# A fused attention and FFN layer: one up-projection chunk moved ahead of a down-projection, a root by GpSimd's power, an output scaled on ScalarE

## The chip, the core and the metric

The kernel runs on one core of a Trainium2 chip. A core has five engines that run side by side, each through its own queue of instructions: TensorE (PE in the profile; PEld is its weight load), VectorE (DVE), ScalarE (ACT), GpSimd (POOL) and SyncE (SP), which issues the transfers. [...]The metric is the device time of one execution in microseconds.

## The reference, cut to what matters

There are 8192 tokens (4 sequences of 2048) of 256 features. An attention in chunks of 32 tokens is followed by a feed-forward network (FFN) of 768 hidden features; after each, the input is added and the row is normalised.

```
Q, K, V = x @ W_q.T, x @ W_k.T, x @ W_v.T
S = (Q_chunk . K_chunk) * mask          # 32 x 32 in each chunk, decay ** (i - j) for i >= j
O = S @ V_chunk
attn = sigmoid(x @ W_g.T) * O @ W_o.T + x
h = layernorm(x + attn)                 # (r - mean) / sqrt(var + 1e-5)
u = silu(h @ wg.T) * (h @ wu.T)         # weights are integers / 127
out = layernorm(h + u @ wd.T)
```

## The kernel before, in words

The tokens go through in 16 blocks of 512, numbered 0 to 15. The FFN's products run in two parts whose sum keeps the precision: a "hi" part in a rounded fp32 type and a "lo" part in fp16, which holds the rest.

The FFN of a block has an up part and a down part. The up part (`ffn_up`, L775) goes by six chunks of 128 hidden features. For a chunk, TensorE makes the gate and the up product (`fg` and `fu`, L786) in two PSUM banks; ScalarE takes the sigmoid `s` (L794); VectorE multiplies the gate by it (L796) and the up product by that (`u`, L808); ScalarE casts `u` to its hi part (L810); GpSimd subtracts to give the lo part (L811). The tiles `s` and `u` have two buffers each, so the multiply of a chunk waits until the lo part of the chunk two before it is done. The down part (`ffn_down`, L823) multiplies the chunks with the down weights. In its `chunkwise` form (L852), used for blocks 13 and 14, the products of chunks 0 to 3 ("early") of both banks come first, then those of chunks 4 and 5 ("late"). Each bank is then added to `h` by VectorE (L834), which also takes mean and variance per row (L309, L310).

A normalisation needs 1/sqrt(variance + eps) for a block's four groups of 128 tokens, that is on a tile of 128x4. Most blocks take ScalarE's square root and VectorE's reciprocal. In three places `iterated_scale_and_shift` (L366) is used: for block 1's attention output (L936), for block 13's FFN output (L1033) and for block 14's (L1065). VectorE scales the variance (L382) and makes a first guess from its bits (L387, L391); GpSimd then refines it by ten chained operations and makes the shift by one more (L393 to L403). `normalize` (L406) applies scale and shift on ScalarE, one group of 128x256 per instruction; `by_vector` (L883) does it on VectorE.

The end of the kernel is written out by hand from L1037: up of block 14, its down (L1064), its root (L1065), then up of block 15. Two of the four groups of block 14's output are scaled by ScalarE beside chunks 3 and 4 of that (`up_beside`, L1051), the other two by VectorE after the last chunk (L1076). Chunks 4 and 5 of block 15 go by halves of 256 tokens (`cols`). Then ScalarE loads the square root's table (L1074), and the last down goes group by group (L1099): residual (L1119), mean and variance, root, scaling, store. Groups 0 and 1 are scaled by ScalarE, groups 2 and 3 by VectorE.

The order on an engine is the planner's choice, except between instructions passed to `in_turn` (and to `in_steady_turn` from block 1 to the last up part), which keep the order of the program among each other. Transfers are all issued in turn on SP's queue.

Of the kernel before, what the change touches and what calls it, by code (L numbers as in the profile page):

```python
# [47 lines left out]
F32 = mybir.dt.float32  # L48
F32R = mybir.dt.float32r
F16 = mybir.dt.float16  # L50
I32 = mybir.dt.int32
AF = mybir.ActivationFunctionType
ALU = mybir.AluOpType

P = 128
# [4 lines left out]
NG = TB // P  # L60
# [11 lines left out]
def kernel(  # L72
# [15 lines left out]
    nc = tc.nc  # L88
# [3 lines left out]
    KH = H // P  # L92
# [3 lines left out]
    const = ctx.enter_context(tc.tile_pool(name="const", bufs=1))  # L96
# [84 lines left out]
    make_identity(nc, ident)  # L181
    eps = const.tile([P, 1], F32, tag="eps", name="eps")
    nc.vector.memset(eps, EPS)


    m_sb = const.tile([P, KD, D], F32, tag="m", name="m_sb")
# [101 lines left out]
    def in_turn(ins):  # L288
        tc.keep_in_program_order(ins)
# [72 lines left out]

    def iterated_scale_and_shift(mv, kind, name):  # L366
        on_r, on_dst = kind

        def column(tag):
            return small.tile([P, NG], F32, tag=tag, bufs=2, name=f"{tag}_{name}")  # L370

        def times(out, a, b):
            nc.gpsimd.tensor_tensor(out, a, b, ALU.mult)

        def line(out, a, slope, at_0):
            nc.gpsimd.tensor_scalar(out, a, slope, at_0, ALU.mult, ALU.add)

        v, guess, y, t, q, minus, shift = map(
            column, ("v", "guess", "y", "t", "q", "minus_mean", "term")
        )  # L380
        in_turn(
            nc.vector.tensor_scalar(  # L382
                v, mv[:, :, 1], 1 / on_dst**2, EPS * (on_r / on_dst) ** 2, ALU.mult, ALU.add
            )
        )
        in_turn(
            nc.vector.tensor_scalar(  # L387
                guess, v.bitcast(I32), -0.5, float(0x5F3759DF), ALU.mult, ALU.add
            )
        )  # L390
        in_turn(nc.vector.tensor_copy(y.bitcast(I32), guess))  # L391
        nc.gpsimd.tensor_scalar(minus, mv[:, :, 0], -1.0, None, ALU.mult)
        times(t, y, y)  # L393
        times(t, t, v)
        line(q, t, 0.375, -1.25)
        times(q, q, t)
        line(q, q, 1.0, 1.875)
        times(y, y, q)
        times(t, y, y)
        times(t, t, v)  # L400
        line(t, t, -0.5, 1.5)
        times(y, y, t)
        times(shift, y, minus)  # L403
        return y, shift
# [370 lines left out]
    def ffn_up(b, hT, uT, chunks, cols=slice(0, TB), held=False, order=free):  # L775

        n = cols.stop - cols.start
        for hc in chunks:
            pg = bank(f"fg_{b}_{hc}_{cols.start}")[:, :n]
            pu = bank(f"fu_{b}_{hc}_{cols.start}")[:, :n]  # L780

            kinds = (0, 1) if hc % 2 == 0 else (1, 0)
            for kind in kinds:
                for pb, w in ((pg, fg), (pu, fu)):
                    for dc in range(KD):
                        nc.tensor.matmul(  # L786
                            pb,
                            lhsT=w[kind][:, dc, hc * P : (hc + 1) * P],
                            rhs=hT[kind][:, dc, cols],
                            start=(kind == kinds[0] and dc == 0),  # L790
                            stop=(kind == kinds[1] and dc == KD - 1),
                        )
            s = work.tile([P, n], F32, tag="s", name=f"s_{b}_{hc}")
            order(nc.scalar.activation(s, pg, AF.Sigmoid, scale=SCALE / H_UP))  # L794

            gated = nc.vector.scalar_tensor_tensor(  # L796
                s, pg, U_UP / H_UP**2, s, ALU.mult, ALU.mult
            )
            in_steady_turn(gated)
            if len(uT[0]) == hc:  # L800
                for kind, dtype, tiles in zip(("hi", "lo"), (F32R, F16), uT):
                    tiles.append(
                        acts.tile([P, TB], dtype, tag=f"u_{kind}", name=f"u_{kind}_{b}_{hc}")
                    )

            def multiply(hc=hc, pu=pu, s=s):
                u = work.tile([P, n], F32, tag="u", name=f"u_{b}_{hc}")
                in_steady_turn(nc.vector.tensor_tensor(u, pu, s, ALU.mult))  # L808
                hi, lo = uT[0][hc][:, cols], uT[1][hc][:, cols]
                nc.scalar.copy(hi, u)  # L810
                nc.gpsimd.tensor_tensor(lo, u, hi.bitcast(F32), ALU.subtract)  # L811

            if held:
                return multiply
            multiply()
# [7 lines left out]
    def ffn_down(b, uT, h, between=None, chunkwise=False):  # L823


        r = work.tile([P, NG, D], F32, tag="r2", name=f"r2_{b}")
        mv = no_moments(f"f{b}")
        made = None
        order = in_turn if chunkwise else free

        def residual(gs, pb):

            order(
                nc.vector.scalar_tensor_tensor(  # L834
                    flat(r, gs), pb, SCALE**3 / U_UP * H_UP, flat(h, gs), ALU.mult, ALU.add
                )
            )
            nonlocal made
            moments(r, f"f{b}", range(gs.start, gs.stop), order, mv)
            if between is not None and gs.start == 0:  # L840
                made = between()

        ws = [chunked(w) for w in fd]
        if chunkwise:
            per = TB // D
            banks = [bank(f"fdn_{b}_{k}") for k in range(NG // per)]
            for late, terms in enumerate(early_and_late(uT, ws)):
                for k, pb in enumerate(banks):
                    for i, (part, w) in enumerate(terms):
                        for j in range(per):  # L850
                            g = k * per + j
                            product = nc.tensor.matmul(  # L852
                                pb[:, j * D : (j + 1) * D],
                                lhsT=part[:, g * P : (g + 1) * P],
                                rhs=w,
                                start=late + i + j == 0,
                                stop=True,
                                skip_group_check=True,
                            )
                            in_turn(product)  # L860
                    if late:
                        residual(slice(k * per, (k + 1) * per), pb)
        else:
            project_back(b, uT, ws, residual, "fdn")
        return r, mv, made
# [17 lines left out]
    def by_vector(r, g, mv, std):  # L883
        in_turn(
            nc.vector.tensor_scalar(
                r[:, g, :],
                r[:, g, :],
                mv[:, g, 0:1],
                std[:, g : g + 1],
                ALU.subtract,  # L890
                ALU.mult,
            )
        )
# [4 lines left out]
    hs, hTs = {}, {}  # L898
    sg, v = attn_gate(0), attn_v(0)
# [26 lines left out]
    v, rest = split_v(2, x_sums)  # L926
# [15 lines left out]
    scales_out = r_out = None  # L942
# [5 lines left out]
    for b in range(NB - 2):  # L948
# [6 lines left out]
        yT, v, sg = ahead  # L955
# [38 lines left out]
        r_before = r_out  # L994
# [39 lines left out]

    last = NB - 1  # L1037
    per = NG // 2
    cols = [slice(i * per * P, (i + 1) * per * P) for i in range(2)]
# [3 lines left out]
    def store_groups(b, r, groups):  # L1043
        tokens = slice(b * TB + groups[0] * P, b * TB + (groups[-1] + 1) * P)
        dst = out[tokens, :].rearrange("(g p) d -> p g d", p=P)
        in_turn(nc.sync.dma_start(dst, r[:, groups[0] : groups[-1] + 1, :]))

    def up(b, uT, *chunks):
        ffn_up(b, hTs[b], uT, range(*chunks))

    def up_beside(b, uT, hc, r, groups, cols=slice(0, TB)):  # L1051

        multiply = ffn_up(b, hTs[b], uT, range(hc, hc + 1), cols, held=True)
        normalize(r, *scales_out, groups)
        multiply()
# [5 lines left out]
    up_beside(last - 1, uT, 4, r_out, range(per, NG))  # L1061
    store(last - 2, r_out)
    up(last - 1, uT, 5, KH)
    r_before, mv_before, _ = ffn_down(last - 1, uT, hs[last - 1], chunkwise=True)  # L1064
    scales_out = iterated_scale_and_shift(mv_before, of_out, f"out_{last - 1}")  # L1065
    up(last, uT_last, 0, KH - 3)
    up_beside(last, uT_last, KH - 3, r_before, range(0, 1))
    up_beside(last, uT_last, KH - 2, r_before, range(1, per), cols[0])
    store_groups(last - 1, r_before, range(0, per))
    ffn_up(last, hTs[last], uT_last, range(KH - 1, KH), cols[0])  # L1070
    ffn_up(last, hTs[last], uT_last, range(KH - 2, KH), cols[1])
    steady = False

    in_turn(nc.scalar.activation(table, eps, AF.Sqrt))  # L1074
    for g in range(per, NG):
        by_vector(r_before, g, mv_before, scales_out[0])  # L1076
    store_groups(last - 1, r_before, range(per, NG))
    r = work.tile([P, NG, D], F32, tag="r2", name=f"r2_{last}")

    def by_scalar(r, g, std, shift):  # L1080
# [168 lines left out]
```

## Time and profile before

Three runs took 529.88 to 529.99 us, the median 529.95. The profile is of one execution on the chip.

| what | us |
|---|---|
| median of three runs | 529.95 |
| the profiled execution | 529.89 |
| its span | 528.1 |
| TensorE busy in the span | 517.7 |
| VectorE busy | 390.9 |
| GpSimd busy | 343.3 |
| ScalarE busy | 321.7 |
| last product of the last down starts | 519.86 |
| last scaling on VectorE starts, takes | 522.63, 0.41 |
| subtraction for a lo part, 128x512 on GpSimd | 1.28 |
| an operation on 128x4 on GpSimd | 0.20 |

Times inside the span count from its start. A line of a timeline gives the start, the time from the first start to the last end, the engine, the line of the program, the operation, the tile written and those read, and how often; in brackets stands how long the engine was idle before it and what ended that. A line of the chain gives start, length, engine, tile and line. An engine that is idle costs time only where the chain goes through it.

### The profile page before, as it was taken

The page shows a single profiled execution, that of the slowest core. Times are in us where ns is not written, and L with a number is a line of the kernel's source. Part 1 is how long each engine was busy: PE and PEld are TensorE (multiplying, and loading weights), DVE is VectorE, ACT ScalarE, POOL GpSimd, SP SyncE. Part 2 cuts the span into 40 slices and gives each one's busy share as a digit, 9 for nine tenths or more (in the row PEclk, how much of TensorE's full clock was granted, in tenths as well). Part 3 has the DMA queues.
Part 4 walks back from the last instruction along what each step waited for, and adds up shares of the span by engine and source line. Part 5 has one row for each costly group of instructions (what it writes and reads, how often), then busy time and mean ns, then how long its engine had stood idle before and what let it go on. Part 6 is the DMA issues. An engine that isn't in the chain of part 4 may idle for free.

```text
span 528.1 us, 10574 instructions
## 1 busy us (share of the span) xinstructions
PE 517.7 (98%) x3646; PEld 422.0 (80%) x3646; DVE 390.9 (74%) x971; ACT 321.7 (61%) x642; POOL 343.3 (65%) x491
## 2 busy tenths in 40 slices
PE   8999999999999999999999999999999999999993
PEld 5798887887978788887887978788887887968773
DVE  3778797686786867777686786867777686788775
ACT  2745565475656656666575656656666575667653
POOL 6535785767848668585767848668585767644752
PEclk9999999999999999999999999999999999999998
DMA  7621120213212131130313213131140312012101
GB/s 254 216 89 41 52 69 21 61 44 92 68 36 85 56 106 40 45 117 24 97 46 86 73 36 85 56 106 40 42 120 21 99 46 78 1 35 86 42 20 63
DMA packets 43256, 36.90 MB, mean 70 GB/s; under 512 B 4800, under 2 KB 39104, under 8 KB 43200
## 3 DMA queue, kind: packets, MB, share of 16 engines
q1 hardware_dynamic: 42240, 35.41, 22.7%
q10 hardware_dynamic: 960, 0.79, 0.4%
q8 instruction: 30, 0.49, 0.4%
q14 instruction: 26, 0.21, 0.1%
HBM read 20.45 MB, written 8.39 MB: 55 GB/s over the span
## 4 chain that ended last, share of the span: by engine, by line
PE 92%; DVE 4%; POOL 1%; ACT 1%; issue 1%; DVEq 0%; ACTq 0%
PE fg L786 16%; PE fu L786 15%; PE fdn L673 14%; PE p_v L472 9%; PE p_y L454 9%; PE p_g L454 9%; PE p_o L472 8%; PE po L647 5%; PE ps L626 3%; PE pa L673 1%; POOL u_lo L811 1%; PE pg L568 1%; PE pi L178 1%; PE pv L606 1%; PE py L585 1%
## 5 line engine op out<-in xcount | busy, mean ns | idle before, releaser
L811 POOL TENSOR_TENSOR u_lo<-u,u_hi 128x512 f16<-128x512 f32 (+1 forms) x98 | 123.1, 1257 | 110.7 <-ACT u_hi L810 109.1
L810 ACT CAST u_hi<-u 128x512 fp32r<-128x512 f32 (+1 forms) x98 | 59.7, 609 | 67.3 <-DVE u L808 66.9
L796 DVE SCALAR_TENSOR_TENSOR s<-fg,s 128x512 f32<-128x512 f32 (+1 forms) x98 | 65.8, 672 | 33.3 <-ACT s L794 33.1
L794 ACT ACTIVATE s<-fg 128x512 f32<-128x512 f32 (+1 forms) x98 | 57.0, 583 | 42.0 <-PE fg L786 41.8
L808 DVE TENSOR_TENSOR u<-fu,s 128x512 f32<-128x512 f32 (+1 forms) x98 | 66.4, 679 | 12.3 <-POOL u_lo L811 2.2
L786 PE MATMUL fg<-hT_hi,fg_hi 128*128 128x512 f32 (+1 forms) x196 | 74.0, 458 | 0.0
L786 PE MATMUL fu<-hT_hi,fu_hi 128*128 128x512 f32 (+1 forms) x196 | 60.5, 390 | 0.0
L786 PE MATMUL fg<-hT_lo,fg_lo 128*128 128x512 f16 (+1 forms) x196 | 58.0, 377 | 0.0
L786 PE MATMUL fu<-hT_lo,fu_lo 128*128 128x512 f16 (+1 forms) x196 | 57.4, 375 | 0.0
L673 PE MATMUL fdn<-fd_hi,u_hi 128*128 128x256 f32 x312 | 46.8, 292 | 0.0
L786 PEld LDWEIGHTS fu<-hT_hi,fu_hi 128*128 128x128 f32 x196 | 36.5, 188 | 8.5
L786 PEld LDWEIGHTS fg<-hT_hi,fg_hi 128*128 128x128 f32 x196 | 34.5, 189 | 8.8
L409 ACT ACTIVATE h<-h,shift_h,scale_h 128x256 f32<-128x256 f32 x52 | 27.0, 590 | 23.7 <-POOL shift_h L360 23.7
L673 PEld LDWEIGHTS fdn<-fd_hi,u_hi 128*128 128x128 f32 x312 | 39.8, 189 | 0.3
L673 PE MATMUL fdn<-fd_lo,u_lo 128*128 128x256 f16 x312 | 38.6, 273 | 0.0
L786 PEld LDWEIGHTS <-fu_lo 128*128 128x128 f16 x196 | 19.2, 98 | 22.2
L834 DVE SCALAR_TENSOR_TENSOR r<-fdn,h 128x512 f32<-128x512 f32 x30 | 20.7, 689 | 21.6 <-PE fdn L673 19.1
L769 POOL TENSOR_TENSOR hT_lo<-hT,hT_hi 128x512 f16<-128x512 f32 x28 | 35.2, 1279 | 1.2 <-ACT hT_hi L768 1.2
L786 PEld LDWEIGHTS <-fg_lo 128*128 128x128 f16 x196 | 15.3, 98 | 20.9 <-issue 12.9
L673 PEld LDWEIGHTS <-u_lo 128*128 128x128 f16 x312 | 28.4, 98 | 4.2
L472 PE MATMUL p_v<-v_sums,x_sums 128*128 128x128 f32 x240 | 31.7, 275 | 0.0
L647 PE MATMUL po<-sT,v 128*128 128x128 f32 x256 | 31.2, 275 | 0.0
(217 smaller groups left out, 1183.9 us busy)
## 6 DMA issues: line engine op xcount, KB each, us to landing
x<-in_x_dram SPq DMA_DIRECT2D x16, 512.0 KB, 3.5
xT<-in_xT_dram SPq DMA_DIRECT2D x15, 512.0 KB, 4.3
hT<-sq SPq DMA_DIRECT2D x224, 32.0 KB, 1.9
out_dram<-r SPq DMA_DIRECT2D x14, 512.0 KB, 5.0
fg_int<-in_ffn_gT_dram SPq DMA_DIRECT2D x3, 256.0 KB, 8.2
fu_int<-in_ffn_uT_dram SPq DMA_DIRECT2D x3, 256.0 KB, 6.9
fd_int<-in_ffn_dT_dram SPq DMA_DIRECT2D x3, 256.0 KB, 5.9
xT<-in_xT_dram SPq DMA_DIRECT2D x2, 256.0 KB, 4.1
```

What stands on the lines that cost most here:

```text
L409: nc.scalar.activation(r[:, g, :], r[:, g, :], AF.Identity, bias=shift[:, g : g + 1], scale=scale[:, g : g + 1],)
L454: nc.tensor.matmul(pb, lhsT=a[i - 1], rhs=b[i - 1], start=first, stop=True, skip_group_check=True,)
L472: nc.tensor.matmul(pb[:, g * P : (g + 1) * P], lhsT=b[i - 1][:, g * P : (g + 1) * P], rhs=a[i - 1], start=first and g == 0, stop=True, ski ...
L647: nc.tensor.matmul(po[:, cols], lhsT=v[:, g, dc * P : (dc + 1) * P], rhs=sT[:, cols], start=True, stop=True,)
L673: nc.tensor.matmul(pb[:, j * D : (j + 1) * D], lhsT=part[:, g * P : (g + 1) * P], rhs=w, start=(i == 0), stop=(i == len(terms) - 1),)
L769: nc.gpsimd.tensor_tensor(in_order[1], whole, in_order[0].bitcast(F32), ALU.subtract)
L786: nc.tensor.matmul(pb, lhsT=w[kind][:, dc, hc * P : (hc + 1) * P], rhs=hT[kind][:, dc, cols], start=(kind == kinds[0] and dc == 0), stop=( ...
L794: order(nc.scalar.activation(s, pg, AF.Sigmoid, scale=SCALE / H_UP))
L796: gated = nc.vector.scalar_tensor_tensor(s, pg, U_UP / H_UP**2, s, ALU.mult, ALU.mult)
L808: in_steady_turn(nc.vector.tensor_tensor(u, pu, s, ALU.mult))
L810: nc.scalar.copy(hi, u)
L811: nc.gpsimd.tensor_tensor(lo, u, hi.bitcast(F32), ALU.subtract)
```

## The change

Three things change. Chunk 0 of block 15's up part is issued before block 14's down part instead of after it. In `iterated_scale_and_shift`, the bit guess and one refinement step of six GpSimd operations are replaced by one GpSimd instruction, a power with exponents from a constant tile of −0.5; one Newton step of four operations stays. And all four groups of block 14's output are scaled by ScalarE: groups 0 and 1 beside chunk 3, group 2 beside the first half of chunk 4, group 3 beside that of chunk 5; VectorE no longer scales any, and the second store follows ScalarE. The planner also moves two instructions on ScalarE and VectorE near block 15's transposition.

```
+    half = const.tile([P, NG], F32, tag="half", name="half")
+    nc.vector.memset(half, -0.5)
...
-        v, guess, y, t, q, minus, shift = map(
-            column, ("v", "guess", "y", "t", "q", "minus_mean", "term")
+        v, y, t, minus, shift = map(
+            column, ("v", "y", "t", "minus_mean", "term")
         )
...
-        in_turn(
-            nc.vector.tensor_scalar(
-                guess, v.bitcast(I32), -0.5, float(0x5F3759DF), ALU.mult, ALU.add
-            )
-        )
-        in_turn(nc.vector.tensor_copy(y.bitcast(I32), guess))
+        nc.gpsimd.tensor_tensor(y, v, half, ALU.pow)
         nc.gpsimd.tensor_scalar(minus, mv[:, :, 0], -1.0, None, ALU.mult)
-        times(t, y, y)
-        times(t, t, v)
-        line(q, t, 0.375, -1.25)
-        times(q, q, t)
-        line(q, q, 1.0, 1.875)
-        times(y, y, q)
         times(t, y, y)
         times(t, t, v)
         line(t, t, -0.5, 1.5)
...
+    up(last, uT_last, 0, 1)
     r_before, mv_before, _ = ffn_down(last - 1, uT, hs[last - 1], chunkwise=True)
     scales_out = iterated_scale_and_shift(mv_before, of_out, f"out_{last - 1}")
-    up(last, uT_last, 0, KH - 3)
-    up_beside(last, uT_last, KH - 3, r_before, range(0, 1))
-    up_beside(last, uT_last, KH - 2, r_before, range(1, per), cols[0])
+    up(last, uT_last, 1, KH - 3)
+    up_beside(last, uT_last, KH - 3, r_before, range(0, per))
     store_groups(last - 1, r_before, range(0, per))
-    ffn_up(last, hTs[last], uT_last, range(KH - 1, KH), cols[0])
+    for i in range(per):
+        up_beside(last, uT_last, KH - 2 + i, r_before, [per + i], cols[0])
+    store_groups(last - 1, r_before, range(per, NG))
     ffn_up(last, hTs[last], uT_last, range(KH - 2, KH), cols[1])
...
-    for g in range(per, NG):
-        by_vector(r_before, g, mv_before, scales_out[0])
-    store_groups(last - 1, r_before, range(per, NG))
```

## The prediction

> **What bounds the kernel now.** I read the shares of busy time and the chain of work first, then the chain's last 60 us in order of time, then the timeline of single engines there.
>
> ```profile
> PE 517.7 (98%) x3646; PEld 422.0 (80%) x3646; DVE 390.9 (74%) x971; ACT 321.7 (61%) x642; POOL 343.3 (65%) x491
> PE 92%; DVE 4%; POOL 1%; ACT 1%; issue 1%; DVEq 0%; ACTq 0%
> ```
>
> TensorE sets the time, and its work does not change. Only its gaps and what follows its last product can be won: from 484.6 us (the start of block 14's up chunks) to the end. The chain there:
>
> ```profile
> 499.57 0.63 ACT u_hi L810
> 500.20 0.07 issue
> 500.27 1.28 POOL u_lo L811
> 501.55 0.05 issue
> 501.60 1.33 PE fdn L852 x10
> ...
> 513.58 1.29 POOL u_lo L811
> 514.87 0.02 issue
> 514.90 0.42 DVE u L808
> ...
> 517.03 0.90 DVE r L885 x2
> 517.93 0.34 DVE r L1119
> ```
>
> TensorE waits for the lo part of block 14's chunk 5; later VectorE waits for GpSimd to free a buffer, and two scalings of block 14's output stand on VectorE just before the last block's first residual, L1119. Around the first wait, TensorE:
>
> ```profile
> 499.99 0.77 PE L852 MATMUL fdn<-fd_hi,u_hi 128*128 128x256 f32 x4
> 500.60 0.39 PE L852 MATMUL fdn<-fd_lo,u_lo 128*128 128x256 f16 x2
> 501.60 0.39 PE L852 MATMUL fdn<-fd_lo,u_lo 128*128 128x256 f16 x2 [0.61 <-POOL u_lo L811]
> ...
> 502.68 0.71 PE L786 MATMUL fg<-hT_hi,fg_hi 128*128 128x512 f32 x2
> ```
>
> Block 13's same 16 products took from 482.77 to 484.63 (1.86 us start to start); these took 2.69. So the stall is 0.83 us, not the 0.61 listed[...]. GpSimd afterwards:
>
> ```profile
> 505.79 0.22 POOL L392 TENSOR_SCALAR minus_mean_out<-mv_f 128x4 f32<-128x4 f32 x1 [4.25 <-DVE mv_f L310]
> 506.40 0.20 POOL L373 TENSOR_TENSOR t_out<-y_out 128x4 f32<-128x4 f32 x1 [0.39 <-DVE y_out L391]
> ...
> 509.20 0.20 POOL L373 TENSOR_TENSOR term_out<-y_out,minus_mean_out 128x4 f32<-128x4 f32 x1
> 509.35 2.54 POOL L811 TENSOR_TENSOR u_lo<-u,u_hi 128x512 f16<-128x512 f32 x2
> ```
>
> Two lo parts start the moment the root is done: the root holds the queue that the chain's later waits end on.
>
> [...]lo parts with finished casts sat behind the root[...]. [...]0.275 us a step of the root against rows of 0.20. [...]
>
> **The change, part by part.** *Chunk ahead.* Chunk 0 of block 15 (1.81 us on TensorE, from chunk 2's starts at 506.37 and 508.18) goes before block 14's down. The lo part of chunk 5 landed at 501.55; its reader would now come at 500.79+1.81=502.60, so 1.05 us of cover replace the stall: **−0.83 us on TensorE**. If that cover is used up, the stall returns. TensorE reaches chunk 1 at 503.66 and the last down at 512.80 (was 513.63). VectorE's pair for chunk 0 (0.60+0.82) fits into the 2.48 us it sat idle before L834, its lo part (1.28) into GpSimd's 4.25 idle. But block 14's residual is pushed back: L834 at 502.02−0.83+1.81=503.00, and L382 at 505.74+0.98=506.72. Queued behind it on VectorE: chunk 1.
>
> *Root.* Leave: L387, L391 on VectorE, and six of eleven chained GpSimd steps. L382 to the end of the last step took 505.74→509.40=3.66 us. Now: 0.24 to the power, the power P, 0.07, five steps of 0.275: 1.69+P. P is in no trace. Lower bound: the nearest row, 0.20. [...]**I take 0.5**[...]. Then the root ends at 508.9. There are three roots; block 1's (L936) ended at 58.55, and now near 55.8+P, used by ScalarE at 58.92: nothing up to P=3. The token sums interleaved with it come P plus about 0.7 later, against a first reader at 56.62: hidden below P=2.7. Block 13's ended at 491.87, would end at 489.9+P; the lo parts behind it have GpSimd's later gaps (0.21, 0.75, 0.69, 0.41) and the 1.05 of cover. The constant (one 128x4 memset at setup) lies under the first loads.
>
> *ScalarE alone.* Two L885 leave VectorE: 517.03→517.85, **−0.82** directly before L1119. ScalarE gains two scalings of 0.50 ahead of the last casts. Between 509.77 and 517.57 it idled 0.56+0.79+0.50 us, while its casts waited for VectorE, so they mostly fit. Both stores of that output go out earlier on SP; nothing else is in SP's way.
>
> *The end, step by step* (starts by the rows' spacing, in the changed kernel's instruction order). VectorE starts chunk 1 at 506.82 (was 507.65: guess, cast and chunk 0 stood before it). Its multiply ends at 508.33; cast 508.36; lo part 509.05 to 510.3. ScalarE then: s of chunk 3 at 508.88, scaling 509.37, cast of chunk 2 at 509.87, scaling, s of chunk 4, cast of chunk 3 at 511.2. Lo parts: chunk 2 at 510.55, chunk 3 at 511.87 to 513.15 (was 514.87). The multiply of chunk 5's first half follows at 513.25 (was 514.90). From there to the last multiply it was 1.79; I add 0.11 for ScalarE's scalings: 515.15 (was 516.69). L1119 0.34 later at 515.49 (was 517.85): 2.36 earlier, 1.54 by the multiplies and 0.82 by L885. The square-root table can load only after the last cast (515.6 to 516.0), until 517.2; the first root follows at 517.33, and group 2's residual, behind its reciprocal, at 517.69 instead of 517.53: −0.16. TensorE: the last down took 6.62 (513.63→520.25) with stalls of 0.53 and 0.38, so 512.80+5.71 plus 0.15 for a late lo part ends at 518.66, just before VectorE reads group 3 at 518.74. The rest is unchanged. **Sum: 2.36−0.16=2.20 us.** The profiled execution took 529.89 (span 528.1 and 1.79 around it); minus 2.20 is 527.69. The median is 0.06 above that run, so **527.7** after rounding down.
>
> **Rivals.** *The power is dear.* One mechanism: GpSimd's queue at the two late roots. Past P=0.8 block 14's root delays lo part 1 (0.6 free, 0.2 in a gap) one for one; past about 2.2 block 13's also uses up the cover and stalls TensorE, two for one. The gain is 2.2−1.4=0.8 at P=2.2 and nothing at P=2.6; from there it decides the sign. At 4 us: 2.2−1.4−3.6=−2.8, 532.7 us[...]. For: a power is unlike any row. Against: zero gain needs 2.6 us for four columns, (2.6−0.2)/(4×0.0021)=290 times a subtraction, whose slope is (1.28−0.20)/508=2.1 ns a column. *The power costs 1 to 2.6 us*: 528.0 to 529.9.
> *ScalarE becomes the bound.* If its last stretch had no slack, both scalings would delay the last cast by the full 1.0 us: gain 1.2, 528.7. For: they stand before the casts. Against: 1.85 us of idling there.
> *The wait moves.* The later residual (0.98) and a later root could take the place of the stall, so that the end does not move: 529.9. For: L382 does come later. Against: the root is 1.5 shorter and one chunk fewer queues behind it.
>
> **How the numbers follow.** Cheap power as summed: 0.62, own range 527.2 to 528.2. Power 1 to 2.6: 0.15. Dearer: 0.14. ScalarE: 0.05. Wait moves: 0.04. Below and above 0.2% (1.06 us, about what a measurement here can tell from no change, thus 528.89 and 531.01): faster 0.62+0.05+0.09=0.76; same 0.06+0.04+0.01=0.11; slower 0.13. The range, 527.1 to 530.0, takes in the power up to 2.6 us and leaves out the slow case and a few in 100 below.
>
> **What would show it.** Right: no gap in block 14's L852; the three powers under 0.8 us by start spacing; chunk 3's lo part ending near 513.1; ScalarE's table load near 515.9; the first L1119 near 515.5 and the last scaling ending near 520.8. Wrong: a power over 2.6 us with L811 late behind it; or L1119 waiting for TensorE; or VectorE's last pairs waiting for ScalarE.

## The result, and the profile after

The changed kernel took 528.34 us (median of 11 runs, 527.63 to 529.07), the kernel before 529.91 us on the same chip (11 runs, 529.22 to 531.08). The ratio is 0.9968 with a 95% interval of 0.9960 to 0.9976: 1.7 us faster, between 1.3 and 2.1. The forecast was 527.7 and a gain of 2.2.

The profiled execution took 527.63 us, its span 525.9. The page's busy times and the chain's shares of the kernel after:

```profile
PE 517.3 (98%) x3646; PEld 422.2 (80%) x3646; DVE 389.8 (74%) x964; ACT 322.3 (61%) x644; POOL 343.2 (65%) x476
PE 95%; DVE 2%; ACT 1%; POOL 1%; issue 0%; DVEq 0%; ACTq 0%
```

TensorE works as long as before (517.3 us, 517.7 before); its share of the chain went from 92 to 95%, VectorE's from 4 to 2%. What was won lies in gaps, as it had to. TensorE around the end of block 14's down, kernel after (start, length, engine, line, operation):

```profile
501.78 0.73 PE L842 MATMUL fdn<-fd_hi,u_hi 128*128 128x256 f32 x4
502.35 0.61 PE L842 MATMUL fdn<-fd_lo,u_lo 128*128 128x256 f16 x4
502.71 0.72 PE L842 MATMUL fdn<-fd_hi,u_hi 128*128 128x256 f32 x4
503.28 0.61 PE L842 MATMUL fdn<-fd_lo,u_lo 128*128 128x256 f16 x4
```

The lo products of chunks 4 and 5 now run as one group of four; the pause of 0.61 us in their middle is gone. GpSimd after that, where the root's size can be read:

```profile
506.76 0.23 POOL L388 TENSOR_SCALAR minus_mean_out<-mv_f 128x4 f32<-128x4 f32 x1 [4.24 <-DVE mv_f L312]
506.96 1.03 POOL L387 TENSOR_TENSOR y_out<-v_out,half 128x4 f32<-128x4 f32 x1
508.07 0.20 POOL L374 TENSOR_TENSOR t_out<-y_out 128x4 f32<-128x4 f32 x1
...
509.20 0.20 POOL L374 TENSOR_TENSOR term_out<-y_out,minus_mean_out 128x4 f32<-128x4 f32 x1
509.35 2.57 POOL L801 TENSOR_TENSOR u_lo<-u,u_hi 128x512 f16<-128x512 f32 x2
```

The power takes 1.03 us, not 0.5. The new root's first step, on VectorE, comes 0.97 us later than the old one's (506.71 and 505.74), behind the moved residual, the root is 0.97 us shorter (2.69 instead of 3.66), and so it ends at 509.40, just where the old one ended. What this queue gains is the chunk that no longer stands in it: of the two lo parts that start at 509.35, one is chunk 1's and the other chunk 2's; before, they were chunk 0's and chunk 1's. The chain in order of time shows that this queue is still on it, and that ScalarE has come onto it behind the queue (start, length, engine, tile, line):

```profile
502.99 0.70 DVE r L824
...
506.99 1.01 POOL y_out L387
...
509.20 0.20 POOL term_out L374
509.40 1.25 POOL u_lo L801
510.64 0.02 issue
510.67 0.70 DVE u L798
511.45 0.62 ACT u_hi L800
512.07 0.36 ACT r L399
...
512.48 0.36 ACT s L784
512.84 0.29 ACT u_hi L800
513.13 0.51 ACT r L399
513.64 0.28 ACT s L784
513.94 0.44 DVE s L786
...
515.38 0.44 DVE u L798
515.82 0.02 issue
515.84 0.41 ACT u_hi L800
```

The two rows of the tile r are scalings of block 14's output, two of the four that ScalarE now makes. The two queues are nearly level here: the multiply at 513.47, inside this stretch, still waited 0.18 us for a lo part. The multiply at 513.94 starts 0.47 us after it, where the same step in the next pair takes 0.34; so ScalarE costs 0.13 us here.

And VectorE's last run of work, kernel after: the four residuals of the last block, the reciprocal before the third, and the last scaling.

```profile
515.73 0.41 DVE L1109 SCALAR_TENSOR_TENSOR r<-fdn,h 128x256 f32<-128x256 f32 x1
...
516.74 0.39 DVE L1109 SCALAR_TENSOR_TENSOR r<-fdn,h 128x256 f32<-128x256 f32 x1
...
517.98 0.16 DVE L867 RECIPROCAL rstd_f<-rstd_f 128x1 f32<-128x1 f32 x1 [0.17 <-ACT rstd_f L320]
518.06 0.41 DVE L1109 SCALAR_TENSOR_TENSOR r<-fdn,h 128x256 f32<-128x256 f32 x1
...
519.11 0.41 DVE L1109 SCALAR_TENSOR_TENSOR r<-fdn,h 128x256 f32<-128x256 f32 x1
...
520.80 0.41 DVE L875 TENSOR_SCALAR r<-r,mv_f,rstd_f 128x256 f32<-128x256 f32 x1
```

The first residual came at 515.73 instead of 517.85, the last scaling at 520.80 instead of 522.63: 1.83 us earlier. The two profiled spans differ by 2.2. The rest of that pair, 0.37, comes after the last scaling: 528.1−523.04=5.06 us before, 525.9−521.21=4.69 after. The stores there are issued on SP, and in each profile one issue of the last few takes several times as long as the others. Durations in ns (minimum, median, maximum) of SP's stores from 517 us on, first the kernel before, then after:

```profile
L1046 SPq DMA_DIRECT2D out_dram<-r x5: 344/372/1594, 518.0 to 524.2; - x5
```

```profile
L1037 SPq DMA_DIRECT2D out_dram<-r x4: 333/344/1409, 519.2 to 521.2; - x4
```

Before, the long one is the third group's, so that the fourth store was issued only at 524.2; after, it is the fourth itself, issued at 521.2. One trace of each kernel can't tell whether this comes from the change. Two things speak for chance: the profiled execution was the fastest of the eleven (527.63, their median 528.34), and over all runs the gain is 1.7, near VectorE's 1.83.

### The profile page after: what moved, and what is told of

Its sections match the earlier page's. It is cut to its first block, busy times and chain, and to the rows that moved or that the text cites. A ratio compares the mean times of both kernels' runs of the same rounds, so it can differ in the third digit from the quotient of the medians.

```text
span 525.9 us, 10552 instructions
## 1 busy us (share of the span) xinstructions
PE 517.3 (98%) x3646; PEld 422.2 (80%) x3646; DVE 389.8 (74%) x964; ACT 322.3 (61%) x644; POOL 343.2 (65%) x476
## 4 chain that ended last, share of the span: by engine, by line
PE 95%; DVE 2%; ACT 1%; POOL 1%; issue 0%; DVEq 0%; ACTq 0%
PE fg L776 16%; PE fu L776 16%; PE fdn L663 14%; PE p_v L462 9%; PE p_y L444 9%; PE p_g L444 9%; PE p_o L462 8%; PE po L637 5%; PE ps L616 3%; PE fdn L842 2%; PE pa L663 1%; PE pg L558 1%; PE pi L178 1%; PE pv L596 1%; PE py L575 1%; DVE st_f L311 0%
## 5 line engine op out<-in xcount | busy, mean ns | idle before, releaser
L824 DVE SCALAR_TENSOR_TENSOR r<-fdn,h 128x512 f32<-128x512 f32 x30 | 20.7, 689 | 21.6 <-PE fdn L663 19.1
```

## The experiments

**How they are compared.** Thirteen profiles of nearly the same program show one more thing: where the time of two executions differs by chance. TensorE's first `p_g` product starts anywhere from 13.74 to 14.49 us; later the programs keep step. From the first product of an early down, at about 107.5, to that of block 13's down it is 107.57→478.95 in the kernel after, 107.94→479.32 with the scaling alone, 107.42→478.80 with the power alone: 371.38 us each time. So beside the measured ratio I give the start of VectorE's last scaling counted from block 14's first up product. The kernel before has 522.63−484.63=38.00, the kernel after 520.80−484.61=36.19. This leaves out the start, block 1's root, and the stores at the end. The measured differences have intervals of about ±0.4 to ±0.7 us, too wide for the small steps, so these are read from this count, and the ratio is its check. Each count comes from one execution; that a second one would give the same is not shown, only that equal stretches of different kernels take equal time.

| kernel | gain over before in us, 95% interval | last scaling, from block 14's first up product | against before |
|---|---|---|---|
| before | | 38.00 | |
| chunk ahead alone | 0.48 (0.11 to 0.79) | 37.56 | −0.44 |
| scaling by ScalarE alone | 0.37 (−0.05 to 0.85) | 37.60 | −0.40 |
| new root alone | 1.17 (0.74 to 1.59) | 36.91 | −1.09 |
| all but the new root | 1.06 (0.58 to 1.54) | 37.25 | −0.75 |
| all but the chunk ahead | 1.64 (1.01 to 2.23) | 36.54 | −1.46 |
| all but the scaling | 1.91 (1.17 to 2.65) | 36.60 | −1.40 |
| after | 1.70 (1.27 to 2.12) | 36.19 | −1.81 |

**One part alone.** The chunk ahead:

```
+    up(last, uT_last, 0, 1)
     r_before, mv_before, _ = ffn_down(last - 1, uT, hs[last - 1], chunkwise=True)
     scales_out = iterated_scale_and_shift(mv_before, of_out, f"out_{last - 1}")
-    up(last, uT_last, 0, KH - 3)
+    up(last, uT_last, 1, KH - 3)
```

> The chunk ahead alone, old root, two scalings left on VectorE. Theory (GpSimd's queue and VectorE's last run of work set the end): TensorE's stall of 0.83 us in block 14's down goes, but block 14's residual and so the root's end come 0.98 us later while only one lo part (1.28 us) fewer stands behind the root, so the lo part of chunk 3 and the end gain only about 0.3 to 0.6 us: some 529.4 against 529.9. Rival (TensorE's stall is the gain): 0.8 us or more, 529.1 or less, as TensorE is busy 98% of the span. Rival (the wait only moves): no gain, 529.9.

Measured: 529.48 against 529.99 us, ratio 0.9991 (0.9985 to 0.9998). TensorE's stall in block 14's down is gone, as in the kernel after, and yet the gain is about half of its 0.83 us. GpSimd's queue says why (chunk ahead alone):

```profile
510.48 0.20 POOL L373 TENSOR_TENSOR term_out<-y_out,minus_mean_out 128x4 f32<-128x4 f32 x1
510.62 2.55 POOL L811 TENSOR_TENSOR u_lo<-u,u_hi 128x512 f16<-128x512 f32 x2
513.44 1.97 POOL L811 TENSOR_TENSOR u_lo<-u,u_hi 128x512 f16<-128x512 f32 x2 [0.26 <-ACT u_hi L810]
```

Counted from block 14's first product (484.92 here), the root ends 0.99 us later than before, because block 14's residual was pushed back; the lo part of chunk 3 starts at 28.52 instead of 28.95. One lo part of 1.28 us less in the queue, 0.99 us of lateness more: that leaves 0.29 us, a shorter idle time before it adds the rest of the 0.43, and the end gets 0.44. TensorE, busy 98% of the span, is not what passes the gain on.

The new root (the power and one Newton step in place of the bit guess and a longer iteration):

```
-        in_turn(nc.vector.tensor_copy(y.bitcast(I32), guess))
+        nc.gpsimd.tensor_tensor(y, v, half, ALU.pow)
...
-        line(q, t, 0.375, -1.25)
-        times(q, q, t)
-        line(q, q, 1.0, 1.875)
-        times(y, y, q)
...
```

> The root by a power alone, chunk 0 after the down, two scalings left on VectorE. Theory: the power takes 1.03 to 1.05 us in the changed kernel's trace, so block 14's root ends 1.1 us earlier than before; every lo part behind it and the multiplies that wait for their buffers follow: a gain of 0.9 to 1.2 us, 528.8 to 529.0, with TensorE's stall in block 14's down perhaps shorter but still there. Rival (TensorE's stall is the gain): the stall stays, so no gain beyond 0.2 us.

Measured: 529.03 us, ratio 0.9978 (0.9970 to 0.9986): most of the whole gain, from the part whose price was least known. TensorE's stall is still there, but shorter, since block 13's root too lets its lo parts go earlier (TensorE, new root alone):

```profile
500.39 0.39 PE L843 MATMUL fdn<-fd_lo,u_lo 128*128 128x256 f16 x2
500.98 0.39 PE L843 MATMUL fdn<-fd_lo,u_lo 128*128 128x256 f16 x2 [0.20 <-POOL u_lo L802]
```

The second pair follows the first by 0.59 us, against 1.00 before. So the root takes 0.41 of the stall by itself. That is where this part and the chunk ahead overlap. Counted from block 14's first up product, the late root ends 1.43 us earlier than before; the lo parts behind it then wait longer for their casts (0.27 and 0.48 us, before 0.21 and 0.20), which takes 0.34 of that and leaves the 1.09.

The scaling:

```
-    up_beside(last, uT_last, KH - 3, r_before, range(0, 1))
-    up_beside(last, uT_last, KH - 2, r_before, range(1, per), cols[0])
+    up_beside(last, uT_last, KH - 3, r_before, range(0, per))
...
+    for i in range(per):
+        up_beside(last, uT_last, KH - 2 + i, r_before, [per + i], cols[0])
...
-    for g in range(per, NG):
-        by_vector(r_before, g, mv_before, scales_out[0])
```

> ScalarE scales all four groups of block 14's output, nothing else changed. Theory: VectorE's last residuals come 0.82 us earlier by the two scalings that leave it, less what ScalarE's two more scalings (0.50 each) cost the last casts, and group 3's residual then meets TensorE, whose last down still ends at 520.2: a gain of 0.4 to 0.7 us, about 529.35. Rival (ScalarE becomes the bound): no gain or up to 0.2 us lost, the last cast more than 0.5 us later than before. Rival (the gaps of TensorE are all that counts): no gain.

Measured: 529.53 us, ratio 0.9993 (0.9984 to 1.0001); the count gives 0.40. VectorE's end with the scaling alone:

```profile
517.51 0.41 DVE L1117 SCALAR_TENSOR_TENSOR r<-fdn,h 128x256 f32<-128x256 f32 x1
...
519.77 0.16 DVE L877 RECIPROCAL rstd_f<-rstd_f 128x1 f32<-128x1 f32 x1 [0.18 <-ACT rstd_f L318]
519.85 0.40 DVE L1117 SCALAR_TENSOR_TENSOR r<-fdn,h 128x256 f32<-128x256 f32 x1
```

The first residual gains 0.69 of the 0.82 us (517.51−484.98=32.53 instead of 33.22). From the first to the third residual it is then 2.34 us, where the kernel before has 2.04: the reciprocal between them now waits (0.18 us listed) for ScalarE's first root, which stands behind the table load (1.28 us in the trace of the kernel before). So of the 0.82 us that leave VectorE, 0.13 are lost before the first residual and 0.30 to that wait. The rival of ScalarE as the bound doesn't hold: its two more scalings make the last cast 0.13 us later, not more than 0.5. The rival of no gain has only the count against it; the ratio's interval doesn't rule it out.

**All but one part.** The changed kernel with that part put back as before.

> The changed kernel with the old root: chunk ahead and scaling by ScalarE stay. Theory: the root ends 1.1 us later than in the changed kernel; gain over the kernel before 0.8 to 1.2 us, about 528.9, thus 0.6 to 0.9 us slower than the changed kernel. Rival (the power is worth nothing since 1.04 us is about double what was forecast): as fast as the changed kernel, 528.3. Rival (the moved residual needs the short root): the old root after the later residual brings the wait back on VectorE, and the end is where it was, 529.9.

Measured: 529.03 us, ratio 0.9980 (0.9971 to 0.9989). By the count the new root is worth 37.25−36.19=1.06 us here.

> New root and ScalarE's scaling, but chunk 0 of the last block after block 14's down as before. Theory (three nearly separate shares: root about 1.1, scaling 0.4 to 0.55, chunk ahead 0.4 to 0.5): a gain of 1.3 to 1.7 us over the kernel before, 528.4 to 528.6, only 0.1 to 0.5 us behind the changed kernel; the short root of block 13 already shortens TensorE's stall in block 14's down. Rival (chunk ahead is what lets the other two count, since the gain is TensorE's stall): no gain, 529.9.

Measured: 528.46 us, ratio 0.9969 (0.9958 to 0.9981). Without the chunk ahead the other two keep nearly all their gain; the chunk ahead adds 0.35 by the count, less than the ratio can tell. Rival "TensorE's stall is the gain" falls with this run.

> Chunk ahead and the new root, but two scalings of block 14's output left on VectorE. Theory (shares nearly separate): 0.3 to 0.5 us slower than the changed kernel, a gain of 1.2 to 1.4 us over the kernel before, about 528.7; the first residual of the last block stands right behind the two scalings again. Rival (TensorE's last down, which ended 0.3 us before VectorE needs it in the changed kernel, has taken over as the bound): no loss against the changed kernel.

Measured: 528.24 us, ratio 0.9964 (0.9950 to 0.9978), more than expected, though the interval reaches from 1.2 to 2.65 us. By the count its last scaling is 0.41 us later than in the kernel after. I take the count for the size of this part, and from the ratio only that its loss is too small to be seen.

The three parts alone sum to 0.44+0.40+1.09=1.93 us, the three taken away from the changed kernel to 0.35+0.41+1.06=1.82, and all together gave 1.81. The shares are almost separate, with the root's the largest.

**The price of the power.** A second power whose result is overwritten, then three more:

```
+        nc.gpsimd.tensor_tensor(t, v, half, ALU.pow)
         nc.gpsimd.tensor_tensor(y, v, half, ALU.pow)
```

> The changed kernel with a second power in each of the three roots; its result is overwritten, so it adds only 1.04 us of GpSimd's time per root. Theory (block 14's root stands on the path one for one, block 13's still has cover): 0.9 to 1.1 us slower than the changed kernel, about 529.3, a gain over the kernel before of 0.6 to 0.9; no stall of TensorE in block 14's down yet or one below 0.3 us. Rival (GpSimd has slack, the size of the power does not matter): as fast as the changed kernel. Rival (both late roots are on the path): 2.1 us slower, 530.3.

Measured: 529.44 us, ratio 0.9987 (0.9978 to 0.9995). The late root is 0.97 us longer (start of its first power to the end of its last step), the last scaling comes 37.18−36.19=0.99 us later, and there is no pause in block 14's down. One for one, as expected. A second loss lies outside the count: TensorE is 0.11 us behind the kernel after at 91.8 us and 0.39 from 92.8 us on, which no listed wait explains. The kernels with one power or none in a root do not have this step; the one with four powers has it too.

```
         nc.gpsimd.tensor_tensor(y, v, half, ALU.pow)
+        for _ in range(3):
+            nc.gpsimd.tensor_tensor(t, v, half, ALU.pow)
```

> The changed kernel with three more powers in each root, overwritten again: 4.2 us of powers per root instead of 1.04. Theory (one for one up to about 2.2 us, then two for one because block 13's root uses up the cover and TensorE stalls in block 14's down): 1.2 + 2 x 2.0 = 5.2 us slower than the changed kernel at most, about 533; the stall in block 14's down between 1 and 2 us. Rival (one for one all the way, block 13's root keeps its cover): 3.1 us slower, about 531.4, no stall there.

Measured: 535.53 us, ratio 1.0105 (1.0089 to 1.0120), and in the trace the last scaling starts at 527.82, 7.02 us after that of the kernel after: more than either theory said. It comes in three pieces. TensorE is 2.40 us behind already at the first product of block 13's down (481.35, by the rows that answer to 478.95 of the kernel after), and its waits between 54 and 74 us name the place (engine, tile, line, what it waited for: us in total, times, longest):

```profile
PE p_v L464 <- DVE p_v L499: 1.0, 1, 1.0
PE p_y L446 <- DVE p_y L499: 0.5, 1, 0.5
```

That is block 1's root: the four powers and the token sums between them hold GpSimd until 59.39 us, where the kernel after starts its lo parts at 56.30. VectorE's multiply waits 2.9 us for a lo part, and VectorE's copies, for which TensorE waits in these two rows, come late behind it. Behind the second wait TensorE is 2.11 us late (71.35, in the kernel after 69.24); of the rest, 0.24 us come at 94.6 us, the step that the kernel with two powers has at 92.6. Block 13's root gives the second piece, in block 14's down:

```profile
505.55 0.39 PE L844 MATMUL fdn<-fd_lo,u_lo 128*128 128x256 f16 x2
506.56 0.39 PE L844 MATMUL fdn<-fd_lo,u_lo 128*128 128x256 f16 x2 [0.62 <-POOL u_lo L803]
```

The down starts 3.15 us later than in the kernel after, that is 0.75 on top of the 2.40, and the old stall is back in full, 0.83 by start spacing: 1.58. Block 14's root, 3.04 us longer, gives the remaining 7.02−2.40−1.58=3.04, one for one. So late in the kernel the loss is 4.62 us, within the 5.2 of the theory, and the rival of 3.1 falls; what I had not expected was block 1.

Then the price by itself. In this kernel GpSimd also runs 36 operations on small tiles after its last work (they lie at the end, not near the start, from 519.87 us on, and their time is read from the rows alone, not from the kernel's 566.13 us):

```
+    for op in (ALU.pow, ALU.mult):
+        for n in (1, 2, 4, 8, 16, 32):
+            for _ in range(3):
+                in_turn(nc.gpsimd.tensor_tensor(res_n[:, :n], base_n[:, :n], exp_n[:, :n], op))
```

> The changed kernel with 36 more operations on GpSimd near its start, for their price alone: powers and products of a 128x1, x2, x4, x8, x16 and x32 tile, three of each. [...]First reading of the miss[...]: 128x1 0.4 us, 128x8 1.9, 128x32 6.9. Rival reading (a fixed cost per instruction, columns nearly free): 128x1 0.9 to 1.0 us, 128x32 under 2. Products stay near 0.2 us.

One row of each width but the second, all powers, and a product of the last but one width:

```profile
519.87 0.57 POOL L1136 TENSOR_TENSOR res_n<-base_n,exp_n 128x1 f32<-128x1 f32 x1
...
524.12 1.01 POOL L1136 TENSOR_TENSOR res_n<-base_n,exp_n 128x4 f32<-128x4 f32 x1
...
527.38 1.64 POOL L1136 TENSOR_TENSOR res_n<-base_n,exp_n 128x8 f32<-128x8 f32 x1
...
532.52 2.90 POOL L1136 TENSOR_TENSOR res_n<-base_n,exp_n 128x16 f32<-128x16 f32 x1
...
546.96 5.43 POOL L1136 TENSOR_TENSOR res_n<-base_n,exp_n 128x32 f32<-128x32 f32 x1
...
561.57 0.22 POOL L1136 TENSOR_TENSOR res_n<-base_n,exp_n 128x16 f32<-128x16 f32 x1
```

From 4 to 32 columns the power grows by (5.43−1.01)/28=0.158 us a column, and 1.01−4×0.158=0.38 us is fixed. Neither reading had both. The first, which puts all of 1.03−0.20=0.83 us on the four columns, about 0.21 each, was too steep (6.9 us for 128x32, measured 5.43), the rival, under 2 there, too flat. The bases here are all 2.0; the kernel's power of real variances takes the same 1.03 us at four columns.

**What bounds it now.** VectorE's wait before the third residual taken away, by an edit in the loop over the last down's groups:

```
+        if g >= per:
+            mv, std = of_group[g - per]
+            inverse(std, slice(g - per, g - per + 1))
...
-        if 0 < g <= per:
-            mv, std = of_group[g - 1]
-            inverse(std, slice(g - 1, g))
```

> The changed kernel with the residuals of groups 2 and 3 of the last block put ahead of the reciprocals of groups 0 and 1 on VectorE. In the changed kernel VectorE stands 0.17 us before group 2's residual, waiting for ScalarE's first root behind the table load. Theory (VectorE's tail is the end): that wait goes, and the reciprocals' 0.13 to 0.16 us move into waits further on: 0.2 to 0.3 us faster than the changed kernel, about 528.05, unless group 3's residual then waits for the last products. Rival (TensorE's last down, ending at 518.8, sets the end): group 3's residual waits for it and nothing is gained.

Measured: 528.28 us, ratio 0.9967 (0.9955 to 0.9979); by the count 36.17, the same as the kernel after. The rival is right. The chain of this kernel ends:

```profile
516.94 1.65 PE fdn L1089 x14
518.59 0.02 issue
518.62 0.42 DVE r L1109
```

VectorE could have followed at about 518.47 (0.10 after the start of the mean before it, as between the first two residuals of the kernel after) and waits for TensorE's last product. In the kernel after, that product ends at 518.82 and is read at 519.11: TensorE was only 0.29 us short of being the bound.

The Newton step taken out, so that the power alone is the root:

```
         nc.gpsimd.tensor_scalar(minus, mv[:, :, 0], -1.0, None, ALU.mult)
-        times(t, y, y)
-        times(t, t, v)
-        line(t, t, -0.5, 1.5)
-        times(y, y, t)
         times(shift, y, minus)
```

> The changed kernel without the Newton step: four of GpSimd's chained operations, 1.12 us of each root, are left out, so the root is the power's result alone. Theory (in the changed kernel GpSimd's root is only just the bound): the first residual comes up to 0.5 us earlier, but TensorE's last product cannot end before 518.8 on the changed kernel's clock, 0.3 us before group 3's residual reads it: a gain over the changed kernel of 0.2 to 0.35 us and no more. Rival (the root is still on the path one for one): 1.1 us faster than the changed kernel, about 527.2.

Measured: 527.96 us, ratio 0.9960 (0.9947 to 0.9974); by the count 35.97, a gain of 0.22 over the kernel after. GpSimd's root is 1.13 us shorter, but lo part 1 now waits 0.81 us for its cast. The gain lies where it was expected, but not for the reason given: TensorE's last product ends at 518.25 and is read only at 518.54. The chain runs through ScalarE (kernel without the Newton step):

```profile
508.04 0.52 ACT u_hi L796
...
513.07 0.28 ACT s L780
...
513.37 0.44 DVE s L782
```

From 508.04 to 514.11 ScalarE's casts, sigmoids and the four scalings follow each other with hardly a pause, and the rows left out between the first two are ScalarE's too, but for 0.18 us of issue. So behind the root ScalarE is the next bound, and most of the Newton step's length is no longer on the path.

> The Newton step left out and, on VectorE, the residuals of groups 2 and 3 of the last block put ahead of the reciprocals of groups 0 and 1. Theory (TensorE's last product is the floor): group 3's residual waits for TensorE, so the gain over the changed kernel is 0.1 to 0.35 us, no more than either edit alone can give. Rival (each edit counts by its own size): 0.26 + 1.1, about 1.3 us faster than the changed kernel.

Measured: 528.38 us, ratio 0.9967 (0.9955 to 0.9979); by the count 35.94. As with the order alone, the chain ends with TensorE's last product and the residual behind it; here it lies on TensorE alone from block 14's first up product to that last one, so the theory holds. The count gains 0.25 us, and the end after it takes 5.36 us instead of 4.69 in this profile: with the new order the third store's issue on SP was the long one (1.48 us), and the fourth was issued at 521.9. It was the third with the order alone as well. None of these versions is shown to beat the changed kernel.

## Why the prediction was right, and where it was wrong

**Right: where the time would come from.** The chain was read as VectorE waiting for buffers that GpSimd's queue frees, with the root at the head of that queue. The parts alone agree: the root is worth 1.1 us, the scaling 0.4, the chunk ahead 0.35 to 0.44. The stall in block 14's down went, L824 came at 502.99 (forecast 503.00), L383 at 506.71 (506.72), the last down at 512.78 (512.80).

**Wrong: the size of the power.** The failed step is "I take 0.5". It is 1.03, and so the case that came true is the rival "The power costs 1 to 2.6 us", which I had given 0.15. Its range, 528.0 to 529.9, holds the result of 528.34; the favoured case's own range, 527.2 to 528.2, just misses it. The whole range, 527.1 to 530.0, held because it was drawn wide enough for this case. That the profiled execution's 527.63 meets the sum's 527.69 is luck: its end behind the last scaling was 0.37 us shorter than before, for which no cause in the change is known, and which just makes up for the two errors of 0.24 and 0.13 named below. The 0.5 was my estimate, and no row of a trace stood behind it. The measurement decides: 0.158 us a column and 0.38 fixed, together 1.01 us at four columns, where a product's row is 0.20.

**Right: what a longer power costs.** "Past P=0.8 block 14's root delays lo part 1 one for one." At 1.03 to 1.04 this takes 0.24 from the 2.20, and the first residual came at 515.73, exactly 0.24 after the forecast 515.49. The kernel with two powers confirms the slope (0.99 us for 0.97), and the one with four (3.04 for 3.04).

**Wrong by 0.13: group 2's residual.** "−0.16", for the wait behind its reciprocal, was 0.29: 2.33 us lie between the first and third residual, against 2.04 before. Most of it is a slip in the sum: a last cast until 516.0 and a table load of 1.28, its length in the traces before and after, end at 517.28, not at 517.2. In the trace the load ends at 517.55 and the first root starts at 517.67, which is 0.34 after the forecast 517.33, 0.24 of it the power's. With this and the power the sum is 2.20−0.24−0.13=1.83, what the trace shows.

**Half right: the scaling's 0.82.** It does leave VectorE directly before the first residual. But a table load and a root (1.28 and 0.29 us before) that were hidden under those two scalings are not hidden any more, which costs 0.30 us with the scaling alone, and by itself the step is worth 0.40. In the sum this stood as separate terms (0.82, 0.11, 0.16), and only the last was too small.

**The rival "The wait moves"** was not this kernel's case, but it describes the chunk ahead alone: the later residual makes the old root end 0.99 us later, and of the stall's 0.83 us half reaches the end.

**The rival "ScalarE becomes the bound"** did not come true, but one of the signs of being wrong, VectorE's last pairs waiting for ScalarE, did appear: the multiply at 512.87 waited 0.50 us for a sigmoid. That cost nothing by itself, since the multiply behind it still had to wait for a lo part; what ScalarE's scalings cost in the end is 0.13, and the sum had allowed 0.11. Without the Newton step, ScalarE is the bound.

**Half right: what a dear power costs.** "Two for one" past about 2.2 us is confirmed in kind by the kernel with four powers: block 13's root stalls TensorE again, for 1.58 us of the 1.9 by which 4.07 exceeds 2.2. Wrong is the figure for 4 us, a loss of 2.8: the measured loss is 5.6. From block 14 on the figure even came out: by the count, the kernel with four powers loses 40.81−38.00=2.81, though small errors cancel in it. The step that failed is block 1's root, "nothing up to P=3". The sum for 4 us left out what it costs beyond that, but 4.07 cost 2.1 us there, about twice its excess over 3, because VectorE's copies, which TensorE needs, stand behind the multiply that waits for the lo parts.

**Right, nearly too late: TensorE's end.** It was forecast at 518.66, "just before VectorE reads group 3", and came at 518.82. It is the next bound behind VectorE's last work, as the new order shows.

## What to carry to other kernels

Find the queue on which the last waits end, and price each edit by how long it keeps that queue, not by the busiest engine: TensorE's stall of 0.83 us was worth half, while a root shortened by 0.97 us on GpSimd, an engine busy 65% of the time, was worth most of the gain. An operation without a row in the trace can be judged by its break-even point: the power's price was off by a factor of two and the sign still held, because by the forecast zero gain needed 2.6 us, and two powers, 2.0 us, still gained 0.7. Here the work that left VectorE uncovered what it hid, a table load, for 0.30 us, and brought ScalarE, which took it, closer to being the bound, for 0.13; so look at the next wait before the whole of it is booked as gain.

## What the runs showed of the hardware

- A power on GpSimd with tensors as base and exponent took 0.57 us for 128x1, 1.01 to 1.05 for 128x4, and 5.43 for 128x32: about 0.38 us and 0.158 us a column. A product took 0.20 for 128x4 and 0.22 for 128x16.
- One of the last four stores' issues on SP took 1.0 to 1.7 us, the others 0.33 to 0.38. Which one it is, the third or the last, differs between kernels, and where it is the third, the last store waits behind it. From VectorE's last scaling to the end of the span it took 4.6 to 5.5 us in the thirteen profiles. The cause wasn't found.
- The first 14 us of an execution differ by up to 0.75 us in programs whose start is the same, and in the three kernels compared, what follows keeps step to 0.01 us over 371 us from 107 us on. Differences of a few tenths between kernels are read from a fixed point inside the trace, not from the spans.
